# Experts' transposes and products in PSUM tiles of their own, a new order of the mixer's opening, and taps loaded by DMA

## The chip, the cores and the metric

The kernel runs on one core of a Trainium2 chip. The metric is the device time of one execution in microseconds. Five engines work side by side, each through its own queue in order: TensorE (PE, with its weight loads shown as PEld), VectorE (DVE), ScalarE (ACT), GpSimd (POOL) and SyncE (SP), which here only issues transfers. They meet through semaphores. SBUF is the working memory; PSUM, 16 KB for each of 128 partitions in eight banks of 2 KB, takes what PE writes.

## The reference

The input is x of 8 x 256 tokens with 128 features. Six sublayers follow one another, each adding to x:

```python
x = x + 0.5 * _L0_ffn_ref(_layernorm(x), ...)   # a cell of six small attentions
x = x + _L0_attn_ref(_layernorm(x), ...)        # attention, 16 heads
x = x + 0.5 * _L0_ffn_ref(_layernorm(x), ...)
x = x + 0.5 * _L1_ffn_ref(_layernorm(x), ...)   # experts, first pass
x = x + _L1_attn_ref(_layernorm(x), ...)        # the mixer
x = x + 0.5 * _L1_ffn_ref(_layernorm(x), ...)   # experts, second pass
```

The change lies in the last three. The experts compute, with eight experts of 64 hidden units and the two best gates of each token kept,

```python
scores = softmax(xf @ gate_w); scale = the two best of 8, others 0
xs = scale.T[:, :, None] * xf[None]
h = silu(xs @ w1) * (xs @ w3); y = (h @ w2).sum over experts
```

The mixer projects x to 256 channels and a gate z, and then has three branches. Two are state space models, one forward and one backward in time (16 states, scan over 256 tokens):

```python
x = silu(causal_dwconv(x, conv_w, conv_b))        # four taps
dt, Bm, Cm = split(x_proj @ x)
delta = softplus(dt_proj @ dt + dt_bias)
h = exp(delta * A) * h + delta * Bm * x           # for each token
y = sum(h * Cm) + D * x;  y * silu(z)
```

The third takes the 2-D Fourier transform of x, convolves real and imaginary parts over frequencies with a filter of five taps (`fft_conv_w`, 512 x 512 x 5), applies silu, transforms back, scales and normalizes. The three are added and projected.

## The kernel before

The tokens are four chunks of 512 (`x[ch]`), each of four tiles of 128. Everything is float32. After the cell, the attention and the second cell comes one program for experts, mixer and experts, `experts_and_mixer` (L800), which the change rewrites in part.

**The order by hand.** This program is a list of slots. `at(slot, f, ...)` (L841) puts a function into a slot's list, `last=True` into a second list behind it; within a list the order is that of the calls of `at`. A loop walks the slots from the lowest to the highest and emits, in each, `scan(i)`, `feed(i+1)`, the first list, `sums`, the second list and `spread(i+2, i+4)`. PE, DVE, ACT and POOL keep exactly this order. SP does not: its transfers are placed by the framework. An instruction waits for the tiles that it reads and writes; a wait goes by whole tile, so two parts of one tile hold each other up.

**Units.** From slot 0 on each slot has one unit of the scan, 32 to a chunk, 128 in all. `spread` (L1156) replicates delta and delta u over the states with matmuls into PSUM tiles `pA` (tag "a", two banks, one buffer) and `pU` (tag "u", two banks, two buffers) and takes the exponential on ACT; `feed` (L1184) multiplies by B on DVE; `scan` (L1191) is the DVE scan and a POOL product with C; `sums` adds up over states in PSUM tag "y" (one bank).

**The bank p.** All other matmuls of the program share one bank, tag "p", one buffer (`bank`, L844). Whoever wants it waits until the last user has been read by ACT or DVE.

**The opening, slots -29 to 0.** Weights are loaded at the program's start, when the cell's memory is free. `taps` (L849, four calls) makes the first projection's weights times each convolution tap: it spreads the tap weights, which lie in columns of `cols`, over 128 columns with matmuls into p, and DVE multiplies into `w["inK"]`. `first.step(n)` (L1017) is one step of the experts' pipeline: `hidden` (L975) of tile n: four matmuls into `ph` (tag "u"), the product with the gates on DVE (`hid`), silu on ACT, a product on POOL; `close` (L1002) of tile n-2: eight matmuls, then x is updated on DVE; `turn` (L994) of tile n-1: four transposes and a copy on ACT. `close` and `turn` use two halves of one tile `pa` (tag "a"). For chunks 1 to 3 `statistics`, `scale`, `transpose`, `logits` and `gates` prepare a chunk; `scale` is called ahead of the step and `transpose` behind it in the same slot, `logits` and `gates` together one slot later. Steps 0 to 11 stand in slots -25 to -14, steps 12 to 17 in slots -10 to -7: a table `lead` says so. In between and around them come the mixer's first inputs: `normalize`, `features`, four `convolve` (L1055, eight PE instructions and an ACT read each) in slots -15 to -12, two `gate`, `silu`, `ranks`, `steps` (L1107) and `softplus`, `delta` (L1130, the sum on DVE, delta u on POOL, two transfers that swap halves).

**The filter.** `fetch` (L884) loads a tap of the filter, 1 MB; `fold_pairs` (L897) adds on POOL and subtracts on DVE two quarters, with one row of 2 KB by transfer; `conv_weights` (L909) is two matmuls (four PE instructions) into p and one ACT copy or two DVE adds. Ten of each run, folding in slots -8 to 1 into three rooms in turn, products in slots -6 to 3.

**The second experts.** The same class. Chunks 0, 1 and 2 are prepared from slots 119, 122 and 125 on, chunk 3 among the steps; steps run in slots 129 to 146. The mixer's last chunk is finished in the first of these (`weigh`, `moments`, `whiten`, `join`, `output`).

Of the kernel before, what the change touches and what calls it, by code (L numbers as in the profile page):

```python
# [17 lines left out]
P = 128  # L18
B, S, D = 8, 256, 128
CT = 512  # L20
# [30 lines left out]
for _name, _n in (  # L51
    ("ew", 18),
    ("act_w", 6),
    ("be", 18),
    ("ln_g", 1),
    ("ln_b", 1),
    ("gamma", 1),
    ("beta", 1),
    ("b_out", 1),
    ("conv_w", 2 * 2 * K),  # L60
    ("conv_b", 4),
    ("dt_b", 4),
    ("Dp", 4),
    ("A_log", 2 * 2 * 4 * 4),
    ("fft_b", 4),
):
    COLS[_name] = slice(_at, _at + _n)
    _at += _n
# [731 lines left out]
def experts_and_mixer(nc, tc, ident, nhalf, x, cols, ins, w, given, store):  # L800
# [19 lines left out]
    with ExitStack() as ctx:  # L820
# [28 lines left out]
        def taps(r, t):  # L849

            pr = bank([P, K, P])
            for k in range(K):
                c = COLS["conv_w"].start + (2 * r + t) * K + k
                nc.tensor.matmul(
                    pr[:, k, :],
                    cols[:, c : c + 1].to_broadcast([P, P]),
                    ident,
                    start=True,
                    stop=True,
                )  # L860
            nc.vector.tensor_tensor(
                w["inK"][:, r, t], pr, bcast(w["inT"][:, t * P : (t + 1) * P], K), ALU.mult
            )
# [33 lines left out]
        def fold_pairs(n, tap, i):  # L897
# [3 lines left out]
            to = fold["room"][:, 1 + n % 3].rearrange("p (k o) -> p k o", k=2)  # L901
# [7 lines left out]
        def conv_weights(tap, i):  # L909

            pw = bank([P, 2 * DI])
            for k in range(2):
                nc.tensor.matmul(
                    pw,
                    fold["fw"][:, int(tap != 2), (1 + i) * k, :],
                    fold["pairs", tap, i][:, k],
                    start=(k == 0),  # L920
                    stop=(k == 1),
                )
            if tap == 2:
                nc.scalar.copy(w["conv"][:, i, tap, :], pw)
            elif tap < 2:
                fold["first", i] = pool.tile([P, 2 * DI], F32, tag="sq", name="first", bufs=2)
                nc.scalar.copy(fold["first", i], pw)
            else:
                first = fold["first", i]
                nc.vector.tensor_tensor(w["conv"][:, i, 4 - tap, :], pw, first, ALU.add)  # L930
                nc.vector.tensor_tensor(w["conv"][:, i, tap, :], pw, first, ALU.subtract)
# [3 lines left out]
        class Experts:  # L935
# [58 lines left out]
            def turn(self, n, pa):  # L994
                if not 0 <= n < NCH * NT:
                    return
                both = self.tiles[n]["both"]
                for k in range(4):
                    nc.tensor.transpose(pa[:, 0, k * P : (k + 1) * P], both[:, 0, k, :], ident)  # L999
                nc.scalar.copy(both[:, 1].rearrange("p k l -> p (k l)"), pa[:, 0, :])  # L1000

            def close(self, n, pa):  # L1002
# [3 lines left out]
                hT = self.tiles[n]["both"][:, 1]  # L1006
                for k in range(4):
                    nc.tensor.matmul(  # L1008
                        pa[:, 1, 0:D], hT[:, k, :], w["w2"][:, k, :], start=(k == 0), stop=(k == 3)
                    )  # L1010
                xt = x[c][:, t, :]
                nc.vector.scalar_tensor_tensor(xt, pa[:, 1, 0:D], 0.5, xt, ALU.mult, ALU.add)  # L1012
# [4 lines left out]
            def step(self, n):  # L1017
                self.hidden(n)
                if 0 <= n - 1 < NCH * NT or 0 <= n - 2 < NCH * NT:
                    pa = ps.tile([P, 2, CT], F32, tag="a", bufs=1, name="pa")  # L1020
                    self.close(n - 2, pa)
                    self.turn(n - 1, pa)
# [398 lines left out]
        first, second = Experts(given=given), Experts(store=store)  # L1421

        lead = dict(zip(range(18), (-25, -24, -23, -22, -21, -20, -19, -18, -17, -16, -15, -14)))
        lead |= dict(zip(range(12, 18), (-10, -9, -8, -8, -7, -7)))
        for n in range(-3, NCH * NT + 2):
            c, i = n // NT + 1, n % NT
            k = lead.get(n, n - 25)
            if 0 < c < NCH and i == 1:
                at(k, first.statistics, c)
            if 0 < c < NCH and i == 2:  # L1430
                at(k, first.scale, c)
            if n >= 0:
                at(k, first.step, n)
            if 0 < c < NCH and i == 2:
                at(k, first.transpose, c)
            if 0 < c < NCH and i == 3:
                at(k, first.logits, c)
                at(k, first.gates, c)
# [11 lines left out]
        for c in range(3):  # L1450
            k = end - 9 + 3 * c
            at(k, second.statistics, c)
            at(k + 1, second.scale, c, room)
            at(k + 2, second.transpose, c)
            at(k + 3, second.logits, c)
            at(k + 4, second.gates, c)
        for n in range(NCH * NT + 2):
            k = n + end + 1
            c = n // NT + 1
            if c == 3 and n % NT == 0:  # L1460
                at(k, second.statistics, c)
            if c == 3 and n % NT == 1:
                at(k, second.scale, c)
            at(k, second.step, n)
            if c == 3 and n % NT == 1:
                at(k, second.transpose, c)
            if c == 3 and n % NT == 2:
                at(k, second.logits, c)
                at(k, second.gates, c)
        at(-29, fetch, None)  # L1470
        at(-29, fetch, 2)
        at(-29, fetch, 0)
        for i in range(4):
            at(-28 + i, taps, i // 2, i % 2)
        at(-20, transform)
        order = [(tap, i) for tap in (2, 0, 4, 1, 3) for i in range(2)]
        for k, (tap, i) in enumerate(order):
            at(-8 + k, fold_pairs, k, tap, i)
            at(-6 + k, conv_weights, tap, i, last=True)
            if i == 1 and k < 6:  # L1480
                at(-8 + k, fetch, order[k + 4][0])

        for ch in range(NCH):

            o = (ch - 1) * UNITS
            if ch == 0:
                for part, k in enumerate((-19, -18, -17, -17)):
                    at(k, normalize, ch, part)
                at(-16, features, ch)
                for i in range(4):  # L1490
                    at(-15 + i, convolve, ch, 1 - i // 2, i % 2)
                at(-11, gate, ch, 0)
                at(-11, gate, ch, 1)
                at(-10, silu, u_of(ch, 0), u_of(ch, 1), sz_of(ch))
                at(-9, ranks, ch, 0)
# [3 lines left out]
                at(-7, steps, ch, 0, 1, last=True)  # L1499
# [21 lines left out]
            at(o + (26 if ch == 0 else 25), delta, ch, 0, 0)  # L1521
            at(o + 26, rows, ch, 0, 1)
            at(o + 26, delta, ch, 0, 1)
            at(o + 28, steps, ch, 1, 0)
            at(o + 29, steps, ch, 1, 1)
# [316 lines left out]
```

## Time and profile before

| what | us |
|---|---|
| median of three runs | 2119.81 |
| lowest and highest | 2116.86, 2122.44 |
| the profiled execution | 2127.31 |
| its span | 2125.5 |
| first instruction of the program's PE work (L854) | 1305.06 |
| first and last scan, start | 1467.22, 2040.99 |
| first `ph` of the second experts, start | 2046.93 |
| last read of the last x, end | 2122.12 |
| a scan; feed; product with C | 2.28; 1.21; 2.35 |
| two units that nothing disturbs, start to start | 3.54 |
| a fold's add on POOL; subtraction on DVE | 1.27; 0.68 |
| mean granted clock | 0.956 |

In a timeline line the first two numbers are start and duration, then come engine, source line, operation, output<-inputs, shapes, the number of instructions merged, and in brackets how long the engine had been idle and who released it. One PE `matmul` call in float32 is two PE instructions. "p", "pa", "ph" are PSUM tiles by their names in the program; `sg_hT` is the tile `both` of a step.

### The profile page before, as it was taken

The numbers are of one execution on the slowest core, as the hardware profiler recorded it, in microseconds if no ns is written. First come the engines' busy times: TensorE is split into PE (matmuls) and PEld (weight loads), VectorE is DVE, ScalarE is ACT, GpSimd is POOL, SyncE is SP. The second block draws the span as 40 slices with busy tenths as digits, with TensorE's granted clock in tenths as the row PEclk, the third lists the DMA queues.
The fourth block names the chain that finished last, engine by engine and source line by source line (L and its number), as shares of the span: only waits on it lengthen the run. The fifth ranks groups of instructions, "written<-read, shape, count | busy, mean of one in ns | idle before, by whom it ended". The sixth has DMA issues, their size and how long they took to land. (4 is left out here: it accounts for less than half of the span.)

```text
span 2125.5 us, 45202 instructions
## 1 busy us (share of the span) xinstructions
PE 1952.2 (92%) x17824; PEld 1129.7 (53%) x17824; DVE 1558.5 (73%) x2669; ACT 1151.2 (54%) x2200; POOL 810.5 (38%) x918
## 2 busy tenths in 40 slices
PE   7999999997999999999999997778788989889887
PEld 5666666654566666666666654532233433334444
DVE  5777777776877776877777785425987978888763
ACT  3777777752332323677777762443355555654543
POOL 3000001036766654100000013314767868778763
PEclk9999999999999999999999997997898999989889
DMA  3000000000000000000000002012000010010000
GB/s 141 3 3 3 3 3 2 3 2 1 2 2 2 2 2 2 2 3 3 3 3 3 3 2 85 1 33 67 1 21 20 1 25 17 4 37 1 1 1 20
DMA packets 21095, 28.19 MB, mean 13 GB/s; under 512 B 12362, under 2 KB 13898, under 8 KB 20244
## 3 DMA queue, kind: packets, MB, share of 16 engines
q1 hardware_dynamic: 20596, 25.11, 4.0%
q8 instruction: 141, 2.31, 0.4%
q14 instruction: 70, 0.57, 0.1%
q10 hardware_dynamic: 288, 0.20, 0.0%
HBM read 15.06 MB, written 1.05 MB: 8 GB/s over the span
## 5 line engine op out<-in xcount | busy, mean ns | idle before, releaser
L345 DVE TENSOR_REDUCE negmax<-sc 128x2 f32<-128x512 f32 x768 | 491.1, 682 | 158.2 <-PE sc L339 157.8
L350 ACT ACTIVATE ex<-sc 128x512 f32<-128x512 f32 x768 | 421.3, 609 | 198.8 <-PE sc L339 198.5
L339 PE MATMUL sc<-qk,qk 32*128 32x256 f32 x6144 | 471.4, 405 | 10.7 <-DVE negmax L345 9.9
L339 PEld LDWEIGHTS sc<-qk,qk 32*128 32x128 f32 x6144 | 295.8, 186 | 147.3 <-ACT ex L350 100.9
L1202 POOL TENSOR_TENSOR hc<-h,C 128x1024 f32<-128x1024 f32 x128 | 301.2, 2357 | 122.4 <-DVE h L1200 117.7
L1200 DVE TENSOR_TENSOR_SCAN h<-dA,pU 128x1024 f32<-128x1024 f32 x128 | 292.1, 2282 | 14.6 <-POOL hc L1202 2.7
L300 ACT ACTIVATE qk<-pp,w_bqk,head_rows 128x256 f32<-128x256 f32 x384 | 197.7, 573 | 73.0 <-PE pp L420 34.7
L86 POOL TENSOR_SCALAR ln_ve<-ln_mv 128x2 f32<-128x2 f32 (+1 forms) x56 | 12.5, 224 | 567.0 <-DVE ln_mv L84 562.1
L1179 ACT ACTIVATE dA<-pA,cols 128x512 f32<-128x512 f32 x256 | 162.1, 684 | 96.4 <-PE pA L1171 95.8
L378 PE MATMUL pc<-ex,va 128*32 128x256 f32 x3072 | 206.0, 386 | 0.2 <-DVE y L443 0.2
L1189 DVE TENSOR_TENSOR pU<-pU,B 128x1024 f32<-128x1024 f32 x128 | 155.7, 1216 | 68.5 <-PE pA L1171 66.2
L1171 PE MATMUL pU<-du,s_sel 32*128 32x512 f32 x512 | 169.5, 682 | 19.8 <-DVE h L1200 19.2
L622 ACT ACTIVATE ex<-sc 128x512 f32<-128x512 f32 x128 | 66.1, 602 | 204.8 <-PE sc L607 204.8
L1171 PE MATMUL pA<-dl,s_sel 32*128 32x512 f32 x512 | 156.6, 687 | 6.3 <-ACT dA L1179 6.3
L607 PE MATMUL sc<-rot,rot 32*128 32x256 f32 x2048 | 135.2, 388 | 1.9 <-POOL rot L590 1.9
L378 PEld LDWEIGHTS pc<-ex,va 128*32 128x32 f32 x3072 | 80.7, 109 | 96.6 <-issue 61.9
L199 POOL TENSOR_SCALAR w_bqk<-pb,head_rows 128x2 f32<-128x2 f32 x12 | 3.5, 313 | 299.0 <-DVE pb L196 292.0
L607 PEld LDWEIGHTS sc<-rot,rot 32*128 32x128 f32 x2048 | 97.9, 184 | 36.8 <-issue 23.0
L625 POOL TENSOR_TENSOR both<-ex 128x512 f32<-128x512 f32 x64 | 80.0, 1271 | 71.2 <-ACT ex L622 71.2
L987 DVE TENSOR_TENSOR hid<-ph,gate 128x1024 f32<-128x1024 f32 x32 | 39.1, 1222 | 90.3 <-PE ph L982 85.3
L1171 PEld LDWEIGHTS pU<-du,s_sel 32*128 32x128 f32 x512 | 47.8, 194 | 99.4 <-issue 78.2
L617 DVE TENSOR_REDUCE anegmax<-sc 128x2 f32<-128x512 f32 x128 | 79.5, 685 | 25.0 <-PE sc L607 25.0
(285 smaller groups left out, 3208.9 us busy)
## 6 DMA issues: line engine op xcount, KB each, us to landing
qk<-turned SPq DMA_DIRECT2D x768, 1.0 KB
s_fft<-s_fft SPq DMA_DIRECT2D x5, 1024.0 KB
du<-ab SPq DMA_DIRECT2D x16, 256.0 KB
B<-low SPq DMA_DIRECT2D x64, 32.0 KB
C<-low SPq DMA_DIRECT2D x64, 32.0 KB
x<-x SPq DMA_DIRECT2D x4, 256.0 KB
out<-x SPq DMA_DIRECT2D x4, 256.0 KB
weT<-ffn_weT SPq DMA_DIRECT2D x1, 960.0 KB
```

The source lines that it names most:

```text
L300: nc.scalar.activation(t[:, g, :], pp, AF.Identity, scale=w["mask"][:, g : g + 1], bias=w["bqk"][:, c, i, g : g + 1],)
L339: nc.tensor.matmul(sc[:, t, :], lhs[:, t * P : (t + 1) * P], rhs, start=True, stop=True)
L345: nc.vector.tensor_reduce(sh[:, :, 4 * g + j], sc, AX.X, ALU.max, negate=True)
L350: nc.scalar.activation(ex, sc, AF.Exp, scale=FD**-0.5)
L378: nc.tensor.matmul(st["pc"][32 * j : 32 * j + 32, g, :], st[2][:, kt, 2 * j + g, :], st["ex", g, j][:, kt, :], start=(kt == 0), stop=(kt = ...
L607: nc.tensor.matmul(sc[j][:, t, :], lhs[r, part, t * P : (t + 1) * P] if part < 2 else sel[r, :], rhs[r, part, :] if part < 2 else st["nm"] ...
L625: nc.gpsimd.tensor_tensor(both, ex[:, :, 0], ex[:, :, 1], ALU.add)
L1171: nc.tensor.matmul(dst[:, jj, :], w["sel"][rs, i, :], src[rs, :], start=True, stop=True)
L1179: nc.scalar.activation(dA[:, jj, :], pA[:, jj, :], AF.Exp, scale=A[:, r, t, i, j : j + 1])
L1189: nc.vector.tensor_tensor(dB, dB, bcast(gots[ch]["B", r], 2), ALU.mult)
L1200: nc.vector.tensor_tensor_scan(hf, af, bf, 0.0, ALU.mult, ALU.add)
L1202: nc.gpsimd.tensor_tensor(hc, h, bcast(gots[ch]["C", r], 2), ALU.mult)
```

## The change

- **Separate PSUM tiles.** `turn` takes a tile `pt` of its own (tag "a"), `close` a tile `po` (tag "y"); `step` is hidden, close, turn in the same order.
- **One row of steps.** `lead` is gone: first steps 0 to 17 stand in slots -24 to -7. `prepare` puts statistics, scale and transpose, logits, gates of a chunk in slots k, k+1, k+2, k+3, the last three in the list behind; as it is called after the steps, `scale` stands behind its slot's step. The mixer's inputs are called before the steps and lie among them: `normalize` at -20 to -17, `features` -16, `convolve` -15 to -12, `gate` -11 and -10, `ranks` -9 and -8, the silus at -13, -11 and -9.
- **Taps by DMA.** `s_inK`, the tap weights spread over 128 partitions and columns by the host's layout (1 MB), is loaded as the second weight; `taps` only multiplies it in place on DVE, in slots -23 to -20. `cols` loses 16 columns. The other weights are loaded in another order.
- **Folding by twos.** `fetch` starts in slot -27. Folds stand in slots -16 to -10, -5, -5 and -4, and go into the three rooms, into buffers of delta and delta u of the second half (tags "dl1", "du1") and two of tag "dA". `conv_weights` takes both halves of a filter tap into a two-bank tile of tag "u" for taps 2, 0, 4, 1 (slots -6 to -3); tap 3 goes singly through p in slots 0 and 1.
- **Delta.** In chunk 0 `steps`, `softplus` and `delta` of the second half come four slots later (slots 0 to 4). In every chunk delta u's transfers of the first half are called ahead of the rows of C.
- **Second experts.** Chunks are prepared from slots 119, 124, 131 and 136 on.

```diff
@@ taps
-            pr = bank([P, K, P])
-            for k in range(K):
-                c = COLS["conv_w"].start + (2 * r + t) * K + k
-                nc.tensor.matmul(
-                    pr[:, k, :],
-                    cols[:, c : c + 1].to_broadcast([P, P]),
-                    ident,
-                    start=True,
-                    stop=True,
-                )
-            nc.vector.tensor_tensor(
-                w["inK"][:, r, t], pr, bcast(w["inT"][:, t * P : (t + 1) * P], K), ALU.mult
-            )
+            to = w["inK"][:, r, t]
+            nc.vector.tensor_tensor(to, to, bcast(w["inT"][:, t * P : (t + 1) * P], K), ALU.mult)
@@ fold_pairs
-            to = fold["room"][:, 1 + n % 3].rearrange("p (k o) -> p k o", k=2)
+            if isinstance(place, int):
+                to = fold["room"][:, place].rearrange("p (k o) -> p k o", k=2)
+            else:
+                to = pool.tile(
+                    [P, 2, 2 * DI], F32, tag=place, name="pairs", bufs=4 if place == "dA" else 1
+                )
@@ conv_weights
-            pw = bank([P, 2 * DI])
+            if len(halves) == 2:
+                pw = ps.tile([P, 2, 2 * DI], F32, tag="u", name="pw")
+            else:
+                pw = bank([P, 1, 2 * DI])
...
@@ turn, close, step
+                pt = ps.tile([P, 4, P], F32, tag="a", bufs=1, name="pt")
...
+                po = ps.tile([P, D], F32, tag="y", bufs=1, name="po")
...
             def step(self, n):
                 self.hidden(n)
-                if 0 <= n - 1 < NCH * NT or 0 <= n - 2 < NCH * NT:
-                    pa = ps.tile([P, 2, CT], F32, tag="a", bufs=1, name="pa")
-                    self.close(n - 2, pa)
-                    self.turn(n - 1, pa)
+                self.close(n - 2)
+                self.turn(n - 1)
@@ the order
+        def prepare(experts, c, k, *room):
+            at(k, experts.statistics, c)
+            at(k + 1, experts.scale, c, *room)
+            at(k + 1, experts.transpose, c, last=True)
+            at(k + 2, experts.logits, c, last=True)
+            at(k + 3, experts.gates, c, last=True)
+        for part, k in enumerate((-20, -18, -19, -17)):
+            at(k, normalize, 0, part)
+        at(-16, features, 0)
+        for i in range(4):
+            at(-15 + i, convolve, 0, 1 - i // 2, i % 2)
+        at(-11, gate, 0, 0)
+        at(-10, gate, 0, 1)
+        at(-9, ranks, 0, 0)
+        for n in range(NCH * NT + 2):
+            at(n - 24, first.step, n)
+        for c in range(1, NCH):
+            prepare(first, c, 4 * c - 28)
...
+        prepare(second, 0, end - 9, room)
+        prepare(second, 1, end - 4, room)
         for n in range(NCH * NT + 2):
+            at(end + 1 + n, second.step, n)
+        prepare(second, 2, end + 3, room)
+        prepare(second, 3, end + 8)
...
+        places = (1, 2, 3, "dl1", "du1", "dA", "dA", 1, 2, 3)
+        slots = (-16, -15, -14, -13, -12, -11, -10, -5, -5, -4)
         for k, (tap, i) in enumerate(order):
+            at(slots[k], fold_pairs, tap, i, places[k], last=True)
             if i == 1 and k < 6:
+                at(slots[k], fetch, order[k + 4][0], last=True)
+        for k, tap in enumerate((2, 0, 4, 1)):
+            at(-6 + k, conv_weights, tap, 0, 1, last=True)
+        at(0, conv_weights, 3, 0, last=True)
+        at(1, conv_weights, 3, 1, last=True)
...
             at(o + (26 if ch == 0 else 25), delta, ch, 0, 0)
+            at(o + 26, delta, ch, 0, 1)
             at(o + 26, rows, ch, 0, 1)
-            at(o + 26, delta, ch, 0, 1)
...
-            at(o - 1, frequencies, ch, 0)
+            at(o - (2 if ch == 0 else 1), frequencies, ch, 0)
@@ the weights
-        w = load(wp, ("inT", "xproj", "dtT", "outT", "FT", "G", "sel", "ysel"), "s_")
+        names = ("inT", "inK", "xproj", "dtT", "sel", "FT", "ysel", "outT", "G")
+        w = load(wp, names, "s_")
```

## The prediction

> **What bounds the kernel now.** I read the page first: its rows by slices show PE at 9 tenths until slice 26 and at 7 or 8 after it, so the part to look at starts near 1300 us, where the mixer program begins. Then the chain that ended last, the timeline from 1290 to 1500 us, and the table by windows for the clock.
>
> The end of the chain, in order of time (start, us, what), shows one step of the second pass of experts:
>
> ```profile
> 2110.80 1.23 DVE hid L987
> 2112.02 0.21 DVE x L1012
> 2112.23 0.14 issue
> 2112.37 0.63 PE pa L999 x4
> 2113.00 1.73 PE ph L982 x4
> ...
> ```
>
> Five links, 4.02 us from one `ph` to the next. The transposes (L999) stand behind a VectorE read of the same tile `pa` (L1012), and that read stands behind the gate product (L987). The engines are not full: PE needs 1.72 for `ph` (2077.83 to 2079.55), 0.86 for the eight products of `close`, 0.47 for the transposes (2081.39 to 2081.86), together 3.05.
>
> The timeline of the opening (start, us, engine, line):
>
> ```profile
> 1305.06 2.08 PE L854 MATMUL p<-ident,cols 128*128 128x128 f32 x8 [0.52 <-DVE y L443]
> ...
> 1318.54 3.12 PE L982 MATMUL ph<-m_w,first 128*128 128x512 f32 x4
> ...
> 1342.42 3.12 PE L982 MATMUL ph<-m_w,xn_xT 128*128 128x512 f32 x4
> ...
> 1375.90 3.71 PE L1063 MATMUL p<-xT,w_inK 128*128 128x512 f32 x8 [0.73 <-ACT xn_xT L964]
> ...
> 1402.91 1.88 PE L982 MATMUL ph<-m_w,xn_xT 128*128 128x512 f32 x4
> ...
> 1426.34 1.12 PE L1114 MATMUL p<-low,s_dtT 64*128 64x512 f32 x2
> ...
> 1431.39 3.75 PE L916 MATMUL p<-fw_pairs 128*128 128x512 f32 x4 [1.45 <-ACT dl L1123]
> ...
> 1467.22 2.28 DVE L1200 TENSOR_TENSOR_SCAN h<-dA,pU 128x1024 f32<-128x1024 f32 x1
> ```
>
> From PE's first free moment (1305.06) to the first scan (1467.22) 162 us pass. The taps come first; the first `ph` is 13.5 late for them. Between 1375.90 and 1402.91 no step runs: convolutions and gates alone, each waiting for ACT to empty the one bank `p`. From 1426.34 the delta chain and the filter products take turns in that bank.
>
> ```profile
> DVE hid L987 <- PE ph L982: 53.5, 12, 16.9
> ...
> PE pa L999 <- DVE x L1012: 12.0, 14, 2.5
> ```
>
> These waits (1310 to 1430 us; total, times, longest) say the same: VectorE idles 16.9 in the hole, and PE waits 14 times for `x`. The windows say what the filter products cost (columns as far as PEclk: PE, PEld, DVE, ACT, POOL busy):
>
> ```profile
> 1430.00:1440.00 10.00, 7.50 (x8) 2.35 (x8) 2.13 (x3) 5.53 (x7) 3.90 (x6) 0.51 0.24 92
> 1440.00:1450.00 10.00, 7.08 (x10) 2.17 (x10) 1.96 (x5) 2.14 (x4) 3.15 (x3) 0.50 0.56 174
> ```
>
> Half clock: four matmuls take 3.75, where they take 1.96 at 1458.80.
>
> **The change, part by part.** Let a be the stretch from 1305.06 to the first `steps` product (L1114, 1426.34), b from there to the first scan, c the first scans, d the end of the scans, e the second experts.
>
> a, 121.3 now. Work on PE, from start-to-start times: sixteen steps of 3.05, 48.8; three chunk transposes of 0.43 and three logits of 0.81, 3.7; transform 1.35; features 0.44; four convolutions of 3.54, 14.2; two gates of 0.97, 1.9; two ranks of 1.71, 3.4. That is 73.8; the 16 tap matmuls are gone. Waits that stay or are new:
> - The first three `ph` on a cold clock as at 1318.54 (3.12 for 1.88): 3.7.
> - The first `hid` can't be written before the old pool is read out (POOL, 1310.05); product 1.23, table load 1.28, silu 0.63, POOL 1.27 bring the first transposes to 1314.75, and PE, done with two `ph` at 1311.3, idles 3.4.
> - New: in the slot where a chunk is scaled, ACT's order becomes silu, copy of the turned tile, scale, where scale stood ahead of the step; the chunk's transposes stand right behind `turn` on PE. So PE waits for copy 0.59, scale 1.65 and hand-overs, 2.6 to 2.9, and about 4.1 for chunk 2, whose four small POOL operations (2.0) come behind a product. All later steps are queued behind that wait. Three chunks, with 0.6 for slower transposes: 10.2.
> - The bank `p` handed on around transform, chunk 3's copy and its logits: 3.2. At the end `close(14)` waits for a copy behind a silu, then for `low`: 2.4. Small remainders 1.9.
> Together 24.8, so L1114 comes at 1403.7, 22.6 earlier. The three scale waits may chill PE: a gap of 2.51 before 1341.54 was followed by a `ph` of 3.12, one of 3.09 before 1364.26 by 2.96, one of 2.29 before 2100.31 by 1.88. By these rows all three cost 1.24 each, 3.7, and the gain is 18.9. The Trainium skill, "TensorE: Matmul & The Clock Gate", section "Why this matters for your kernels", warns only of idle gaps over some 3 us, and so against the wait of chunk 2 alone; by it the sum would be 2.5 better. The trace has a cold `ph` after 2.51 already, so I keep the rows. Bounds: 26 (half of the new waits hidden) and 10 (a third of the PE work cold, 12 more).
>
> The taps' multiplies stay (0.69 each, VectorE), hidden by steps that wait for PE. Their 1 MB is a new transfer on SyncE's queue, second of the weights: at the 351 GB/s of 1320 to 1325 us it takes 3 us, so it lands by about 1316 (s_inT was issued at 1310.08 and used at 1313.07), and all behind it 3 us later, with chunks of time to spare. The third `hid` (about 1322) stands behind the first multiply; were the transfer late, that is the first to slip. The 16 columns that `cols` loses are 8 KB of a transfer long before.
>
> b, 40.9 now. From L1114 (0): ACT's Abs and Relu twice, to 4.9; table load and two Exp/Ln, 8.4; sum on VectorE, 9.6; product on POOL (2.72), 12.4; the du transfers land at 17.2 (ACT's wait for them ended at 1443.58). PE meanwhile: second L1114 to 3.6, then pairs of filter products, 3.5 each in two-bank tiles, to 7.1, 10.6, 14.1; pA(0), 15.2; the fourth pair, 18.7; pA(1), frequencies, 20.9; the next spread waits for dA(1), 22.4; feed 1.22; scan at 24. The first pair starts cold as at 1431.39, 2 more: gain 14.9. If all four run cold (7.2 each) the gain is 2.1; with none, 16.9. Folding's ten adds (1.27, POOL) and subtractions (0.68, VectorE) move into slots with 6.5 us of PE work and cost nothing there; without that cover each slot has 2.54 of POOL against 3.05 of PE, still covered.
>
> c: units 0 to 6 take 30.5 for 21.2 undisturbed. Eight products leave, but two `steps` of delta's second half (PE 1.12, ACT 1.27 each in bank `p`), softplus and delta come in. In slots 0 to 2 I count 19.7 of bank hand-overs for 10.6: the same 9. Taken as 0; 4 better if no VectorE add is waited for, 6 worse if each hand-over takes another scan's 2.28. The delta DMAs put ahead of the C rows (eight issues, 4.97) change nothing in later chunks: the rows left at 1569.63, du at 1588.45, when POOL was ready.
>
> d: chunk 2's statistics 1.65, logits 0.4 and gates 2.2 leave VectorE in scans 125 to 129: 4.25. Chunks 0 and 1 now transpose in the slot of their scale, which holds up a spread by 1 or so each: 2 net, from -2 to 4.2.
>
> e: chunk 2's preparation now lies among steps 2 to 5; its POOL part pushes whiten, join and the mixer's last product, so `ph` 6 comes 1.0 later against the first `ph`. Then nine steps: 27.5, scale wait 3.1, transposes and logits 1.24, gates and table load on the chain 1.0, together 32.8 for 39.0 (2073.81 to 2112.83). The last tile: 8.35 for 9.3, its transposes no longer behind `x`. Less 1.2 of cold clock: 5, from 0 (4.02 stays) to 9 (no scale wait).
>
> Sum: 18.9 + 14.9 + 0 + 2 + 5 = 40.8. The profiled execution took 2127.3 (span 2125.5), 7.5 above the median of 2119.81; it becomes 2086.5, and the median 2079.
>
> **Rivals.** Row transfers in the way. The SyncE queue issues 32 rows of B and C at 0.62, 20 us in all; a folded pair's row 128 and du go through the same queue. In the trace SyncE split C's rows around a pair's row, which speaks against; eight rows ahead of each of the two would cost up to 12: 2091.
>
> Steps stay at 4.02, because another wait (POOL's product, 0.36 of slack by my count) takes the place of `x`: sixteen times 0.97, less the waits that it absorbs, 8, and e's 5: 2092.
>
> The new waits cost less than counted, since the convolutions lie among them: a at its 26, e at 9, c at 2: 2066.
>
> The other side: a cold clock. From 1305 to the first scan PE has 95 us of work (73.8 and 21). At half clock throughout that is 95 more; waits of 30 would absorb some and 9 is already counted: 2079 + 56 = 2135. It decides from 50 us of uncovered cold work. For it: 0.50 to 0.62 between 1430 and 1460. Against: 0.83 to 1.00 in every window of 1340 to 1430, with steps looser than the new ones.
>
> **How the numbers follow.** Forecast 0.58 (2070 to 2090 by itself), rows 0.14, steps 0.12, fewer waits 0.11, cold clock 0.05. Leaving out the cold clock and the ends of the bounds gives 2060 to 2102. Within 0.3% (6.4 us) is what a measurement of this kernel can't tell from no change. Only the cold clock ends slower, part of the first two rivals at their worst near no change: 0.93 faster, 0.02 same, 0.05 slower.
>
> **What would show it.** First `ph` at 1305 and no L854; `ph` to `ph` near 3.1 in the last steps, with PE waits for ACT's scaled chunk in place of those for `x`; no stretch without steps in the convolutions; L1114 near 1407 and the first scan near 1433; clock near 1 in the filter products. Wrong it goes if PE waits for POOL in each step, or fw_pairs' transfers appear as releasers of L916.

## The result and the profile after

The changed kernel takes 2087.49 us (median of four runs, 2081.01 to 2090.59); the kernel before took 2121.09 beside it (2116.86 to 2122.44). The ratio is 0.9841, with a 95% interval of 0.9813 to 0.9869: 33.6 us faster. The forecast was 2079, 8.5 too low; the measured time lies inside its range of 2060 to 2102.

The profiled execution took 2090.59 (span 2088.8). In its timeline of the opening (start, us, engine, line, in brackets the idle time before and who ended it) the first `ph` stands at 1306.51 and no tap product is left:

```profile
1306.51 6.45 PE L980 MATMUL ph<-m_w,first 128*128 128x512 f32 x8 [0.52 <-DVE y L442]
1316.17 1.11 PE L998 MATMUL pt<-ident,sg_hT 128*128 128x128 f32 x4 [3.21 <-POOL sg_hT L989]
...
1341.06 1.48 PE L961 MATMUL p<-ident,xn_xT 128*128 128x128 f32 x4 [2.50 <-ACT xn_xT L116]
1342.37 3.19 PE L980 MATMUL ph<-m_w,xn_xT 128*128 128x512 f32 x4
...
1367.53 6.66 PE L1061 MATMUL p<-xT,s_inK 128*128 128x512 f32 x8 [0.68 <-ACT xn_xT L962]
1374.03 1.88 PE L980 MATMUL ph<-m_w,xn_xT 128*128 128x512 f32 x4
...
1409.74 1.12 PE L1112 MATMUL p<-low,s_dtT 64*128 64x512 f32 x2
...
1413.27 5.42 PE L913 MATMUL pw<-fw_pairs 128*128 128x512 f32 x12
...
1433.49 2.29 DVE L1198 TENSOR_TENSOR_SCAN h<-dA,pU 128x1024 f32<-128x1024 f32 x1
```

Steps go on among the convolutions, and the filter products run at full clock: twelve in 5.42 us. The first `steps` product (now L1112) has moved from 1426.34 to 1409.74, the first scan from 1467.22 to 1433.49. New are the chunk transposes (L961) that wait for ACT, and a lower clock behind each of these waits: `ph` takes 3.62 at 1320.52 and 3.19 at 1342.37 for 1.88, the convolution at 1367.53 takes 6.66 for 3.71.

The waits from 1310 to 1430 (total, times, longest) hold no wait of PE for `x` any more. VectorE still waits 42.9 us for `ph`, 22.7 of it (6.13, 5.12 and 11.44) for the three `ph` behind the chunk waits:

```profile
DVE hid L985 <- PE ph L980: 42.9, 12, 11.4
...
PE p L961 <- ACT xn_xT L116: 5.9, 3, 2.5
```

The table by windows (length, busy time of PE, PEld, DVE, ACT and POOL, then PEclk) has the filter products at 1.00; the low clock, 0.67 on average, is now in the first scans:

```profile
1415.00:1425.00 10.00, 10.00 (x26) 4.09 (x25) 6.87 (x6) 5.15 (x8) 5.50 (x7) 1.00 0.20 46
...
1441.00:1451.00 10.00, 7.70 (x26) 2.41 (x18) 4.95 (x5) 3.01 (x5) 2.35 (x1) 0.67 0.00 0
```

In the chain that ended last a step of the second experts is PE alone, 3.04 us from `ph` to `ph`, where it was five links and 4.02:

```profile
2071.43 1.72 PE ph L980 x4
2073.14 0.89 PE po L1008 x8
2074.03 0.44 PE pt L998 x4
2074.47 1.72 PE ph L980 x4
```

Against the forecast's terms, profiled execution against profiled execution:

| stretch | forecast gain | measured | how |
|---|---|---|---|
| a, to the first `steps` product | 18.9 | 16.6 | 1426.34 to 1409.74 |
| b, from there to the first scan | 14.9 | 17.1 | 40.88 to 23.75 |
| c, units 0 to 6 | 0 | -3.4 | 30.48 to 33.85 |
| units 6 to 120 | not in it | -1.8 | 502.27 to 504.08 |
| d, end of the scans to the first `ph` | 2 | 2.3 | 41.02 to 39.68, and 5.94 to 4.98 |
| e, second experts | 5 | 5.9 | rest of the span, 78.57 to 72.72 |
| sum | 40.8 | 36.7 | spans 2125.5 and 2088.8 |

### The profile page after: what moved, and what is told of

Its sections match the earlier page's. It is cut to its first block, busy times and chain, and to the rows that moved or that the text cites. A ratio compares the mean times of both kernels' runs of the same rounds, so it can differ in the third digit from the quotient of the medians.

```text
span 2088.8 us, 45123 instructions
## 1 busy us (share of the span) xinstructions
PE 1946.3 (93%) x17792; PEld 1127.5 (54%) x17792; DVE 1564.9 (75%) x2669; ACT 1151.7 (55%) x2202; POOL 812.7 (39%) x918
## 3 DMA queue, kind: packets, MB, share of 16 engines
HBM read 16.10 MB, written 1.05 MB: 8 GB/s over the span
## 5 line engine op out<-in xcount | busy, mean ns | idle before, releaser
L1187 DVE TENSOR_TENSOR pU<-pU,B 128x1024 f32<-128x1024 f32 x128 | 155.7, 1216 | 76.5 <-PE pA L1169 72.4
```

What stands on the lines that cost most here:

```text
L1187: nc.vector.tensor_tensor(dB, dB, bcast(gots[ch]["B", r], 2), ALU.mult)
```

## Experiments

Theory: the shared tile sets the step, and the new waits for a scaled chunk, with the cold clock behind them, are what the new order pays. Rivals: another wait takes the place of x, and the waits merely move. Times are medians; each ratio is to the kernel before on the same chip; the stretches are those of each kernel's one profiled execution.

| run | us | ratio and 95% interval | first `ph` | a from there | b | c | units 6 to 127 | last scan to end |
|---|---|---|---|---|---|---|---|---|
| before (profiled) | 2121.09 | | 1318.54 | 107.8 | 40.9 | 30.5 | 543.3 | 84.5 |
| changed | 2087.49 | 0.9841 (0.9813 to 0.9869) | 1306.51 | 103.2 | 23.8 | 33.9 | 543.8 | 77.7 |
| b_tiles | 2107.06 | 0.9924 (0.9898 to 0.9950) | 1318.08 | 97.1 | 38.7 | 30.5 | 543.2 | 75.7 |
| b_dma | 2124.67 | 1.0006 (0.9993 to 1.0018) | 1307.91 | 117.8 | 40.8 | 30.5 | 543.2 | 84.4 |
| b_tiles_dma | 2098.80 | 0.9871 (0.9850 to 0.9891) | 1305.09 | 101.6 | 39.7 | 30.5 | 543.8 | 75.2 |
| a_shared | 2103.25 | 0.9904 (0.9884 to 0.9924) | 1303.14 | 114.4 | 25.4 | 31.5 | 539.3 | 87.4 |
| a_scale | 2079.89 | 0.9795 (0.9773 to 0.9817) | 1305.19 | 96.3 | 23.8 | 31.5 | 543.1 | 77.3 |
| a_both | 2073.28 | 0.9760 (0.9743 to 0.9777) | 1307.68 | 93.8 | 25.5 | 30.6 | 543.8 | 70.9 |
| a_tap3_pair | 2075.04 | 0.9773 (0.9744 to 0.9802) | 1306.59 | 98.4 | 31.6 | 23.4 | 537.7 | 77.7 |
| a_delta | 2079.22 | 0.9795 (0.9770 to 0.9821) | 1302.83 | 98.8 | 30.3 | 23.5 | 542.0 | 78.0 |
| a_single | 2095.65 | 0.9875 (0.9855 to 0.9896) | 1307.92 | 98.5 | 35.3 | 38.4 | 536.0 | 77.8 |
| a_rows | 2087.39 | 0.9816 (0.9795 to 0.9836) | 1307.28 | 99.8 | 25.4 | 31.6 | 542.8 | 77.7 |
| a_best | 2073.01 | 0.9749 (0.9728 to 0.9770) | 1307.68 | 93.6 | 29.9 | 24.5 | 545.2 | 70.9 |
| a_best_late | 2069.16 | 0.9731 (0.9700 to 0.9762) | 1307.71 | 93.8 | 25.5 | 25.1 | 542.5 | 70.9 |

The kernel before read 2121.09, 2122.30, 2124.11 and 2126.51 beside the four groups of runs, so kernels of different groups are compared by ratios: the first row of runs stands alone, the first group is b_tiles, b_dma, a_shared and a_scale, the second a_both, a_tap3_pair, a_single and a_delta, the last the other four. In a_rows the engines run the changed kernel's instructions in the same order (below), so it is a second reading of the changed kernel: 0.9816 (0.9795 to 0.9836) for 0.9841, with b 25.4 for 23.8 and c 31.6 for 33.9. A gain over the changed kernel counts as shown here only if it also stands against a_rows.

### b_tiles: the separate tiles alone

```diff
 class Experts (kernel before)
-                pa = ps.tile([P, 2, CT], F32, tag="a", bufs=1, name="pa")
-                self.close(n - 2, pa)
-                self.turn(n - 1, pa)
+                self.close(n - 2)
+                self.turn(n - 1)
...
+                pt = ps.tile([P, 4, P], F32, tag="a", bufs=1, name="pt")
+                po = ps.tile([P, D], F32, tag="y", bufs=1, name="po")
```

> The kernel before with one part of the change: the transposes in a PSUM tile of their own, the products in another. Theory (the shared tile sets the step): in the last steps of the second experts ph follows ph after about 3.05 us instead of 4.02, PE no longer waits for x, ph(6) to ph(15) falls from 39.0 to about 30, and the opening loses some 5 to 8 of its 12.0 us of waits for x: 14 to 17 us faster in all. Rival (POOL's product takes the place of x): steps stay at 3.7 to 4.0 with PE waiting for ACT or POOL, at most 4 us faster.

Measured: ratio 0.9924, 15.2 us, as the theory has it. The end of its chain is PE alone, as in the changed kernel, 3.05 us from `ph` to `ph` (start, us, what):

```profile
2085.73 1.72 PE ph L982 x4
...
2088.78 1.72 PE ph L982 x4
```

The last stretch falls from 84.5 to 75.7. In the opening the gain was larger than expected, 10.7 from the first `ph` to the first `steps` product. POOL's product did not take the place of x.

### a_shared: that part undone

```diff
 class Experts (changed kernel)
-                self.close(n - 2)
-                self.turn(n - 1)
+                pa = ps.tile([P, 2, CT], F32, tag="a", bufs=1, name="pa")
+                self.close(n - 2, pa)
+                self.turn(n - 1, pa)
```

> The changed kernel with transposes and products back in one PSUM tile, all else as changed. Theory (the separate tiles are worth about as much in either order): last steps at 4.02 again, PE waits for x again; 9 us back in the second experts and 5 to 8 in the opening, 13 to 17 us slower than the changed kernel. Rival (in the new order the waits for ACT's scaled chunk and the convolutions between the steps absorb the waits for x): only the plain steps at the end pay, 5 to 7 us slower than the changed kernel.

Measured: 2103.25, 15.8 us above the changed kernel's median, which is the theory. The waits from 2010 us on (total, times, longest) are back:

```profile
PE pa L997 <- DVE x L1010: 9.3, 13, 0.8
```

From 1300 to 1420 they take another 8.8 in 12. So the new order does not absorb them: the tiles are worth 13 to 16 us in either order (0.9904 less 0.9841, and 1 less 0.9924, of 2121; with 0.9816 for the changed kernel the first is 19).

### b_dma and b_tiles_dma: the taps by DMA

Both also load the weights in the changed kernel's order.

```diff
 b_dma (kernel before)
-            pr = bank([P, K, P])
-            ... four products with ident ...
-            nc.vector.tensor_tensor(w["inK"][:, r, t], pr, bcast(...), ALU.mult)
+            to = w["inK"][:, r, t]
+            nc.vector.tensor_tensor(to, to, bcast(w["inT"][:, t * P : (t + 1) * P], K), ALU.mult)
 b_tiles_dma: this, the tiles of b_tiles, and
-            at(-28 + i, taps, i // 2, i % 2)
+            at(-23 + i, taps, i // 2, i % 2)
```

> The kernel before with one part of the change: the filter taps come spread out by a DMA, the 16 tap products are gone. Theory: the first ph comes about 13 us earlier, an idle of some 3.4 us appears behind the first hid, and 9 to 10 us of it arrive at the first scan and at the end. Rival: the stretch without steps (27 us among the convolutions, paced by ACT emptying p) and the delta chain are reached earlier but the gain is used up in new waits there: 0 to 4 us faster.

Measured: ratio 1.0006. Nothing arrives, and not for the rival's reason: the gain is gone before the convolutions. The timeline of b_dma shows where:

```profile
1313.32 0.43 SPq L1614 DMA_DIRECT2D s_inK<-s_inK  x1
...
1318.79 1.90 DVE L852 TENSOR_TENSOR s_inK<-s_inK,s_inT 128x512 f32<-128x512 f32 x3 [7.48 <-issue]
...
1320.60 1.22 DVE L976 TENSOR_TENSOR hid<-ph,gate 128x1024 f32<-128x1024 f32 x1
...
1325.29 1.12 PE L988 MATMUL pa<-ident,sg_hT 128*128 128x128 f32 x4 [11.00 <-POOL sg_hT L980]
```

The first `ph` stands at 1307.91, but its `hid` is queued on VectorE behind three multiplications of taps, and these start 5.47 after the transfer was issued. PE then waits 11.0 where the changed kernel waits 3.21. With the multiplications moved behind the first steps:

> The kernel before with two parts of the change: separate tiles, and the taps by DMA with their multiplications in slots -23 to -20, behind the first hid and not ahead of it; the rows of work as before. Theory (the DMA alone brought nothing because its multiplications stood ahead of the first hid on VectorE and waited 5.5 us from issue to landing): the first hid comes near 1312, 7 to 10 us more than with the tiles alone reach the first scan and the end, 2097 to 2100 us. Rival (the stretch without steps in the convolutions takes it up): as with the tiles alone, 2104 to 2108 us.

Measured: 0.9871 against 0.9924 for the tiles alone, 11 us of 2121; 2098.80, inside the theory's span. The first scan comes 7.4 earlier (1453.88 to 1446.45). So the DMA pays with the later slots of `taps`. The two runs differ in the tiles too, and the later slots without the separate tiles were not run; that the early slots lose the gain is read from the trace above, at the first transposes, where no `x` is waited for.

### a_scale and a_both: the new waits

```diff
 a_scale (changed kernel)
-            at(k + 1, experts.scale, c, *room)          # in prepare, behind the steps
+        for c in range(1, NCH):
+            at(4 * c - 27, first.scale, c)              # ahead of the steps
+        for c, k in enumerate((-8, -3, 4, 9)):
+            at(end + k, second.scale, c, *((room,) if c < 3 else ()))
 a_both: this, and
-            at(k, experts.statistics, c)
+            at(k - 1, experts.statistics, c)
```

> The changed kernel, but the scaling of a chunk stands ahead of the step of its slot on ACT, not behind it. Theory (the new waits are what the forecast charged 10.2 and 3.1 us for): the waits of PE's chunk transposes for the scaled chunk (1.81, 2.50, 1.59 in the opening, 1.07 and 1.59 in the second experts) go, and with them the slow products behind them (a ph of 3.62 and one of 3.19, a convolution of 6.5 instead of 3.5, a ph of 3.40): 8 to 13 us faster than the changed kernel. Rival (the scaling only pushes silu, and with it POOL's product and the next step's transposes, by its 1.65): each chunk gains a little and loses it one step later, 0 to 3 us faster.

Measured: 0.9795 against 0.9841, 7.6 us by the medians: between the two, next to the theory. Against a_rows (0.9816) it is 4.5 us with intervals that overlap, so the total alone does not show it. Only chunk 3's wait in the opening went. For chunks 1 and 2 the scaling now waits for POOL, as the timeline of a_scale shows:

```profile
1316.60 0.24 POOL L108 TENSOR_SCALAR ln_shift<-ln_shift 128x4 f32<-128x4 f32 x1
1316.87 1.65 ACT L116 ACTIVATE xn_xT<-x,ln_shift,ln_rs 128x128 f32<-128x128 f32 x4 [3.43 <-POOL ln_shift L108]
...
1317.42 1.63 PE L961 MATMUL p<-ident,xn_xT 128*128 128x128 f32 x4 [1.46 <-ACT xn_xT L116]
...
1360.35 0.60 PE L961 MATMUL p<-ident,xn_xT 128*128 128x128 f32 x4
```

At 1360.35 chunk 3, whose POOL work was done in time, is transposed without a wait and at full clock. The second experts took 77.3 for 77.7: chunk 3 there still waits 1.6, for POOL too.

> The changed kernel with a chunk's statistics one slot earlier and its scaling ahead of the step, so two slots instead of one from the statistics to the scaling. Theory (with the scaling alone moved, the four small operations of POOL behind a product became the last thing waited for): the remaining waits of PE for the scaled chunk (1.46 and 1.69 in the opening, 0.5 and 1.6 in the second experts) go, the slow products behind them too (3.08, 3.17 and 3.37 for 1.88, transposes of 1.5 to 1.6 for 0.6): 6 to 10 us faster than with the scaling alone moved, 13 to 17 us faster than the changed kernel. Rival (POOL's operations now stand ahead of a product of the slot before, and PE waits for that product instead): 0 to 2 us faster than with the scaling alone moved.

Measured: 0.9760, 14.2 us less than the changed kernel by the medians (17 by the ratios, 12 against a_rows, with intervals apart from both): the theory in size. In the last steps of a_both nothing waits and nothing is slow:

```profile
2041.15 0.60 PE L961 MATMUL p<-ident,xn_xT 128*128 128x128 f32 x4
2041.59 1.88 PE L980 MATMUL ph<-m_w,exT 128*128 128x512 f32 x4
```

The last stretch falls from 77.7 to 70.9; 2.9 of the 6.8 is paid in units 118 to 126, 54.2 us for 51.2, where two chunks' statistics now stand a slot earlier (units 121, 125 and 126 grew; why was not isolated). In the opening one wait grew: chunk 1's statistics now come ahead of the first `hid`, the first transposes wait 4.92 for 3.21, and a `ph` of 3.18 is left behind them.

### a_tap3_pair, a_delta and a_single: who uses bank p in the first scans

```diff
 a_tap3_pair (changed kernel)
-        for k, tap in enumerate((2, 0, 4, 1)):
+        for k, tap in enumerate((2, 0, 4, 1, 3)):
             at(-6 + k, conv_weights, tap, 0, 1, last=True)
-        at(0, conv_weights, 3, 0, last=True)
-        at(1, conv_weights, 3, 1, last=True)
 a_delta
-            v = o + 4 * (ch == 0)
+            v = o
 a_single: the loop and the two lines above become
+        for k, (tap, i) in enumerate(order):
+            at(-6 + k, conv_weights, tap, i, last=True)
```

> The changed kernel, but the last two filter products (tap 3) are made as a pair in delta u's tiles in slot -2, not singly in bank p in slots 0 and 1. Theory (the two single products, their hand-overs of p and the half clock behind them are what units 0 to 2 lose): units 0 to 6 fall from 33.85 us to 25 to 27, the first scan comes 3 to 4 later, 3 to 5 us faster in all. Rival (the two steps products of delta's second half and ACT's work on them pace slots 0 to 2): units 0 to 6 take 30 or more, the end comes 0 to 4 us later than in the changed kernel.

> The changed kernel with delta's second half four slots earlier, where it was before, the filter products in pairs as changed. Theory (it needs only bank p, which the pairs left free): the first scan comes 2 to 4 us later, units 0 to 6 take 4 to 6 less, 0 to 3 us faster in all. Rival (its work on ACT and VectorE stands ahead of the copies and sums of the filter products): the first scan comes 6 or more later, units 0 to 6 gain no more than 4, the end 2 to 5 us later.

In the changed kernel the two single products of tap 3 take turns in p with the two `steps` products of delta's second half, and run at a lower clock (both take 1.96 in a_both):

```profile
1437.37 2.77 PE L913 MATMUL p<-fw_pairs 128*128 128x512 f32 x4 [1.65 <-ACT dl L1121]
...
1441.96 1.12 PE L1112 MATMUL p<-low,s_dtT 64*128 64x512 f32 x2
...
1446.04 3.75 PE L913 MATMUL p<-fw_pairs 128*128 128x512 f32 x4 [0.77 <-ACT xT L1041]
```

Either of the two taken away leaves c at 23.4 or 23.5 us instead of 33.9, or of 30.6 to 31.6 in the four other kernels that keep both there (a_both, a_scale, a_shared, a_rows). So it is the meeting of both in p that costs, some 7 us in a_both where the two products run at full clock, and not one of them: the rival of a_tap3_pair falls. But most of this is moved and not won. From the first `steps` product to unit 12 (b and the first twelve units) the changed kernel takes 78.9, a_tap3_pair 76.3 and a_delta 75.1: 2.6 and 3.8 us. By the same instructions that stretch took 76.5 in a_scale and 78.3 in a_rows, so the 2.6 is not shown, and of the 3.8 only 1.4 lies outside that spread. a_delta's first scan came 6.6 later, the rival's size, but c fell by 10.4, more than either side had said. a_tap3_pair's first scan came 7.9 later in b and not the 3 to 4 expected: its pair also makes `feed` wait behind four VectorE operations (1432.82 to 1435.22), and 2.7 are the clock, since the first twelve filter products, the same in both kernels, took 8.15 for 5.42. The medians are 12.4 and 8.3 us below the changed kernel's, the ratio of a_tap3_pair with an interval apart from it but not from that of a_rows. The rest lies in stretches that the edits do not touch: the opening took 98.4 and 98.8 for 103.2, and units 12 to 120, the same instructions in all three, 476.7 and 479.7 for 482.8. Since the instructions are the same, this is no gain of the edits; a part of it is the clock (below), the rest stays open.

> The changed kernel with the filter products back singly in bank p, one in each slot from -6 to 3, the delta chain's second half where the change put it. Theory (the pairs are what the stretch from the first steps product to the first scan gained): that stretch goes from 23.75 us to 33 or more, at half clock again, and units 0 to 6 to 35 or more; 10 to 15 us slower than the changed kernel. Rival (that stretch gained because delta's second half left it): 24 to 28 us for it, 2 to 6 us slower in all.

Measured: 0.9875, 8.2 us above the changed kernel's median, between the two (13 by the ratio to a_rows, the theory's size). Folding kept its changed slots here, so two of the ten folded inputs (tap 2's second half, tap 0's first) are written over by tap 3's before they are multiplied; those two products use other data, and one waits for it:

```profile
1422.87 3.69 PE L913 MATMUL p<-fw_pairs 128*128 128x512 f32 x4 [7.07 <-POOL fw_pairs L897]
```

Less these 7.07 the stretch b is 28.2, at the edge of the rival. What the pairs alone are worth in b is therefore not settled by this run. A bound comes from a_delta: with pairs, the new folding and delta's second half where it was, b is 30.3 for 40.9, so 10.6 of b's gain of 17.1 does not need delta's move. In c the single products cost 4.5 more than in the changed kernel (38.4 for 33.9), as the theory has it.

### a_rows: the transfers' order

```diff
-            at(o + 26, delta, ch, 0, 1)
             at(o + 26, rows, ch, 0, 1)
+            at(o + 26, delta, ch, 0, 1)
```

> The changed kernel with the eight C row transfers of each delta ahead of delta u's two on SyncE's queue, as before the change. Theory (PE reaches the first spread only 5.2 us after du has landed, so 5.0 us of issues are covered): first scan within 1 us of the changed kernel's 23.75 from the first steps product, total within 3 us of it. Rival (transfers of rows stand in the way of du): first scan 3 to 5 us later, and as much again in each later chunk's turn, up to 12 us slower.

Measured: 2087.39, b 25.4 us. The run decides nothing between the two: SyncE's queue kept its order, since the framework places these transfers and not the list. The timeline of a_rows:

```profile
1410.92 6.79 PE L913 MATMUL pw<-fw_pairs 128*128 128x512 f32 x12
...
1419.85 0.51 SPq L1137 DMA_DIRECT2D du<-ab  x1
...
1423.57 5.01 SPq L1103 DMA_DIRECT2D C<-low  x8
```

What it does show is that swapping the two calls is no change, and the spread of b by the same order, 23.8 and 25.4: the first twelve filter products took 6.79 here, at a clock of 0.55 from 1410.9 to 1414, and 5.42 in the changed kernel at 1.00. Rows ahead of du were not tried.

### a_best and a_best_late: the repairs together

```diff
 a_best: a_both and a_tap3_pair
 a_best_late: a_both, and
-        at(0, conv_weights, 3, 0, last=True)
-        at(1, conv_weights, 3, 1, last=True)
+        at(8, conv_weights, 3, 0, last=True)
+        at(9, conv_weights, 3, 1, last=True)
```

> The changed kernel with statistics a slot earlier, scaling ahead of the step, and tap 3 as a pair in slot -2. Theory (the two repairs lie in different stretches and add up): against the kernel with the first repair alone the stretch to the first scan takes 6 more and the scans 12 to 14 less, 5 to 9 us faster than it, 2064 to 2068 us. Rival (what the pair saved was in part the clock's chance, the opening of that run being 5 us shorter than that of the changed kernel by the same code): 0 to 3 us faster, 2070 to 2073 us.

> The changed kernel with statistics a slot earlier, scaling ahead of the step, and tap 3's two products still single in bank p but in slots 8 and 9 instead of 0 and 1. Theory (bank p is only fought over while delta's second half uses it too, since either of the two alone left units 0 to 6 at 23.4 to 23.5 us): the first scan stays at 25.5 us from the first steps product, units 0 to 6 take 23 to 24, units 8 to 10 some 2 to 4 more than 7.1; 4 to 8 us faster than without the move, 2065 to 2069 us. Rival (a single product in p among scans costs the same wherever it stands): units 8 to 10 take 13 or more, 2071 to 2075 us.

Measured: 0.9749 and 0.9731 against 0.9760 for a_both. Both beat the kernel before and the changed one; their intervals overlap that of a_both, so the second repair is not shown by the totals. From the first `steps` product to unit 12, a_both takes 77.3, a_best 75.7, a_best_late 73.7: 1.6 and 3.6 us, where the same instructions spread from 76.5 to 78.9 in other runs. For a_best this is the rival's small gain. For a_best_late b stayed at 25.5 as the theory has it; c is 25.1, and units 8 to 10 take 9.0 for 7.1, where the rival had 13. The fastest kernel of the study is a_best_late at 2069.16, by its ratio 1.1% of the kernel before under the changed kernel, and 0.85% under a_rows, read beside it.

## Why the prediction was right, and where it was off

**Steps.** Right: 3.05 forecast, 3.04 to 3.05 measured, and the rival of POOL's product fell in b_tiles. The last nine steps of the second experts with chunk 3's preparation took 33.1, a `ph` of 3.40 at 2056.56 within it, for the forecast 32.8 and 1.2 of cold clock; the last tile took 8.16 for 8.35.

**a.** 16.6 for 18.9. 1.45 of the difference is no part of the change: in this execution the program's first `ph` came at 1306.51, not at 1305.06. By itself a took 103.2, but 98.4, 98.8, 98.5 and 99.8 in a_tap3_pair, a_delta, a_single and a_rows, whose opening is the same code; with those, a would be 20.0 to 21.5. The idle behind the first `hid` was 3.21 (forecast 3.4).

The waits for a scaled chunk were taken as "Three chunks, with 0.6 for slower transposes: 10.2". PE waited 1.81, 2.50 and 1.59, in all 5.9, and then its transposes took 1.64, 1.48 and 1.50 for 0.60, 2.8 more. These are one wait: the scaling is four ACT instructions, 1.65 in all, and the weight load of each transpose waits for the next of them, 0.38 after the one before. The granted clock over the second of these groups was 1.00 (timeline, and its row of the table by windows, columns as above):

```profile
1341.44 0.14 PEld L961 LDWEIGHTS p<-ident,xn_xT 128*128 128x128 f32 x1 [0.24 <-ACT xn_xT L116]
1341.82 0.14 PEld L961 LDWEIGHTS p<-ident,xn_xT 128*128 128x128 f32 x1 [0.25 <-ACT xn_xT L116]
...
1341.00:1342.40 1.40, 1.18 (x5) 0.61 (x6) 0.00 (x0) 1.15 (x4) 1.23 (x3) 1.00 0.00 0
```

So charging the whole scaling to PE was right, and the term measured 8.7 for 10.2; half of the rest is chunk 2, 3.4 for some 4.1: its POOL operations ended at 1340.16, before ACT came to the scaling at 1340.51. Once the scaling stands earlier, as in a_scale, POOL's operations are what it waits for, and for chunk 1 too, where the working had named chunk 2 only. The term of the cold clock, "all three cost 1.24 each, 3.7", was too small: `ph` 3.19 for 1.88 and the products of `close` behind it 1.47 for 1.05 are 1.7, those at 1323.93 with 1.91 0.9, the convolution 6.66 for 3.71 3.0; together 5.6. The two errors cancel by luck: 14.3 for 13.9. Besides, the lower bound of a was reckoned too mildly: a third of 73.8 us of work at half clock would cost 24.6 more and not 12. The measured 16.6 stayed away from it.

**b.** 17.1 for 14.9: "The first pair starts cold as at 1431.39, 2 more" did not happen in this execution, where the windows read 1.00 from 1409 to 1433. That was luck: the same twelve products took 5.42 in the changed kernel and in a_scale, but 6.79 in a_rows, 6.95 in a_shared and 8.15 in a_tap3_pair. With the b of a_rows the gain is 15.5, near the forecast.

**c.** "Taken as 0" was 3.4 off in this execution and 0.2 to 1.2 in a_both, a_scale, a_shared and a_rows (30.6 to 31.6). The count of hand-overs saw that the bank stays as busy as before. Five users of p in slots 0 and 1 leave gaps of 1.65 and 1.53 on PE; the two products of tap 3 behind such gaps took 2.77 and 3.75 here and 1.96 each in a_both, where c is 30.6. So the 3.4 is in the main the clock, which the term left out. Nor did it ask what the two pieces of work would cost apart: 7 less.

**d and e.** 2.3 for 2, 5.9 for 5. That chunk 2 delays step 6 was right in kind: `ph`(6) comes 1.3 later against the first `ph`, for 1.0.

**The total.** 2087.5 for 2079. The terms give 36.7 for 40.8, 4.1 less. The other 4.4 is the offset from profile to median: the sum subtracted all of the 7.5 by which the profiled execution of before stood above its median of 2119.81, but that of the changed kernel stands only 3.1 above its own.

**The other rivals.** The cold clock would have needed 50 us of uncovered cold work; PEclk from 1305 to 1430 is 0.89 in both kernels. Fewer waits: 8.7 for 10.2 in the opening, but with more cold clock behind them. Row transfers: the trace of the changed kernel has du's issue at 1422.21 and C's at 1425.93, so nothing stood in the way.

**What is worth what.** By ratios: tiles alone 0.76%, tiles and DMA 1.29%, the whole change 1.59%. The rest of the change brings some 0.3%, with intervals that overlap; by a_rows (1.84%), read in the same group as tiles and DMA, it brings 0.55%, with intervals apart. Its new order gains in b and pays in the chunk waits and in c; with the waits repaired it brings 1.1% (1.29% to 2.40% in a_both).

## What to carry over

Where two engines take turns in one PSUM tile and waits go by whole tile, read the chain for the link that only the sharing makes; two tiles were worth some 15 us of 2121 here, in either order. A transfer in place of computed data pays only if the instruction that reads it does not stand ahead of the critical one in its queue: the same DMA was worth nothing in slot -28 and, with the separate tiles, 11 us in slot -23. When a preparation moves into the steps, follow its whole chain (statistics, small POOL operations, scaling, transposes) through each queue and leave a slot between the links; moving only the last link left half of the waits. Before a slow matmul is put down to the clock, look at what its weight loads wait for and at the granted clock of its window. And read one order twice before small gains are believed.

## What the runs showed of the hardware

A wait of PE far below 3 us can be followed by a lower granted clock, and is not always. The plainest place is a `steps` product of chunk 1 in the scans, behind a single wait of 1.59 or 1.60. In the changed kernel it took 2.03 us, with a clock of 0.54 from 1564.5 to 1566.7:

```profile
1564.59 2.03 PE L1112 MATMUL p<-low,s_dtT 64*128 64x512 f32 x2 [1.59 <-ACT dl L1121]
```

In a_tap3_pair it took 1.12, with a clock of 1.00 from 1555.9 to 1557.2:

```profile
1555.99 1.12 PE L1112 MATMUL p<-low,s_dtT 64*128 64x512 f32 x2 [1.60 <-ACT dl L1121]
```

It took 2.07 in a_rows and a_scale, behind 1.58 and 1.59, and 1.12 in a_both, behind 1.59. The first filter products, behind a wait of 1.36 and one `steps` product, are another (5.42 to 8.15 us for the same twelve).

The chunk waits of the opening are a third, but a less clean one: in the 3.8 us ahead of the convolution (1363.77 to 1367.53 in the changed kernel) PE did nothing but four transposes of 0.60 in all. In five kernels the convolution came behind the same two waits of 1.59 and 0.68; in the changed kernel it ran for 6.66 us at a clock of 0.54, in a_tap3_pair (its timeline here), a_delta, a_single and a_rows for 3.71:

```profile
1365.70 3.71 PE L1061 MATMUL p<-xT,s_inK 128*128 128x512 f32 x8 [0.68 <-ACT xn_xT L962]
```

The forecast had kept the rows against the rule of the Trainium skill, "TensorE: Matmul & The Clock Gate", section "Why this matters for your kernels", that only idle gaps over some 3 us matter. In the changed kernel slow products stood behind each of the three waits, all below 3 us, though ahead of the first the clock was already at 0.50 (1316 to 1319). So keeping the rows came nearer than dropping them; a_rows, where the convolution was not slow, shows that not every such wait costs something. The same page's section "What's actually happening" says that the activity window runs freely and is not tied to the kernel's start; that the same code met it differently from run to run fits, but no run here shows the window itself.

Units 12 to 120 of the scans are the same instructions in seven kernels (the changed one, a_shared, a_scale, a_tap3_pair, a_delta, a_single, a_rows) and took 475.1 to 482.8 us; the opening by the same code took 98.4 to 103.2 in five. By these, a single profile of this kernel is uncertain by some 5 us in the opening and 8 in the scans, and differences of that size between totals were read with their intervals or left open.
